# Layer 3 feed-forward: a PSUM pair of its own for the query and key projections, a pinned place for VectorE's rotation, and more, smaller unit parts

## The chip, the cores and the metric

The kernel runs on one core of one Trainium2 chip. The metric is the device time of the whole kernel in microseconds (us); lower is better. The time before is the median of three runs, 2732.9 us, and the three lie between 2726.75 and 2735.28 us. One execution was profiled; it took 2729.0 us, of which 2726.9 us lie between the first and the last instruction (its span).

The engines are named as in the profile: PE is TensorE's matmuls, PEld its weight loads, DVE is VectorE, ACT is ScalarE, POOL is GpSimd, SP is SyncE, which issues DMAs.

## What is computed

The reference is a small network of four layers, each made of a feed-forward block, an attention block and the feed-forward block again. All is float32, with 4 sequences of 512 tokens and 128 features. Only layer 3's feed-forward block is changed. It is itself two transformer layers (`DEPTH = 2`), and it is called twice, before and after layer 3's attention:

```python
def _layer(x, wqkv, qs, ksc, wo, lg, lb, w1, b1, w2, b2):
    h = shift_token(x)                       # upper 64 features come from the token before
    q, k, v = jnp.split(h @ wqkv, 3, axis=-1)    # 8 heads of 64
    q = l2norm(q) * qs; k = l2norm(k) * ksc
    q, k = rotary_xpos(q, k)                 # q * cos * scale + rotate_half(q) * sin * scale
    x = x + local_attention(q, k, v) @ wo    # windows of 64 keys and the 64 before them
    h = shift_token(x)
    h = (h - mean) / sqrt(var + 1e-05) * lg + lb
    a, g = jnp.split(h @ w1 + b1, 2, axis=-1)    # 341 hidden features each
    return x + (a * gelu(g)) @ w2 + b2
```

## The kernel before

`l3_ffn` (lines 1593 to 1901) is one long software pipeline. A **unit** is one of the two transformer layers for one of the four sequences, so a call has 8 units. A **step** is one block of 128 tokens of a unit, so a unit has 4 steps (`TB`) and a call has 32. The loop at lines 1878 to 1886 goes over step numbers n. In each turn it traces six **stages**, each for an older step than the stage before it:

| place | stage | step | what it does |
|---|---|---|---|
| 0 | `project` (1643) | n | PE: q and k into a pair of PSUM banks `p_qk`, v into one bank `pv`. ACT: squares `sq`, copy `v`. DVE: q and k times the cosine table (`t1`, line 1661), two half products with the sine table (`t2`, line 1664), sums of squares `rn` (1666). POOL: inverse root of `rn` (ten small instructions, lines 195 to 205), `t1 + t2` (1668), k times its inverse norm (1669). SP: two DMAs that shift v by half a block (`vb`) |
| 1 | `to_features` (1681) | n - 2 | PE: 8 transposes into a pair `pt_qk`. ACT copies the q half (`qT`), DVE the k half (`kT`, 1693) |
| 2 | `exponentials` (1722) | n - 4 | ACT: 8 exponentials over `s`. DVE: reciprocal `sm`. POOL: `s` times `sm` (1731) |
| 3 | `weights` (1698) | n - 3 | PE: scores into a pair `ps3`. DVE: mask (`s`, 1714), row maximum `nm` (1716) and its scaling (1719) |
| 4 | `turn_weights` (1733) | n - 5 | PE: 8 transposes into a pair `pt3`. ACT copies them (`PT`) |
| 5 | `with_values` (1742) | n - 6 | PE: weights times values into one bank `po3`. DVE copies it (`oT`, 1757) |

The rest of a unit, from the output projection to the second linear layer, is cut into **parts** that are hung between the stages of later steps. `parts` (lines 1867 to 1871) gives for each the step, counted from the unit's first, and the place ahead of which it is traced. `attended`: output projection `pz`, added to `yT` by DVE (1773), then `shift`, which is one copy on ACT and one on DVE into `h2`. `mean`: product `pm`, subtraction on DVE (1782), square on ACT. `variance`: product `pvar`, copy `rs` on DVE (1793), then an inverse root of ten instructions on POOL. `spread`: `rs` into a diagonal matrix `dg` on DVE (1801). `normed`: product `pb` of `dg`, then `h2` scaled on DVE (1811). `hidden` 0, 1 and 2: each two products into a pair `pag`, a GELU on ACT and a product `hh` on DVE (1824). `close_unit`: product `pz2`, added to `yT` on DVE (1836). `leave`: back to token order.

Three things set the order of the work:

- **Pins.** Every PE and ACT instruction of this block goes through `tc.keep_in_program_order`, which places it behind the instruction traced last on the same engine. So PE and ACT run in the order of the code. DVE and POOL instructions of this block are not pinned: a scheduler lays them out when the kernel is compiled, the earliest traced first among those that it takes to be ready. On the chip every engine then works through its own list in order, and an instruction that waits holds up what stands behind it.
- **PSUM rings.** PSUM has 8 banks. `banks(tag + "ps", d=3, m=2)` makes a ring of three pairs for tag `d` (`p_qk`, `pt_qk`, `ps3`, `pt3`, `pag`, in the order of the code) and a ring of two single banks for tag `m` (`pv3`, `pz`, `pm`, `pvar`, `pb3`, `po3` and so on). A product into a ring of three waits until the pair used three before it has been read.
- **Ticks.** Work that other blocks left over is run a piece at a time by `tick()` once after each stage.

Steps 10 to 13 of a call carry the parts of unit 0, steps 14 to 17 those of unit 1, and so on; steps 0 to 9 carry none, and after step 31 only the later stages go on. The last unit's parts follow the loop (`rest`, line 1888), in the second call in two halves.

Of the kernel before, what the change touches and what calls it, by code (L numbers as in the profile page):

```python
# [23 lines left out]
F32, I32 = mybir.dt.float32, mybir.dt.int32  # L24
AF = mybir.ActivationFunctionType
ALU = mybir.AluOpType
AX = mybir.AxisListType

P = 128
# [74 lines left out]
def tile_macaron(ctx, tc, x_in, const_in, vec_in, w0_in, ws_in, ws3_in, w2f_in, w3_in, out):  # L104
    nc = tc.nc
    pool = lambda name, **kw: tc.tile_pool(name=name, bufs=1, **kw)
# [9 lines left out]
    @contextmanager  # L116
    def banks(name, **bufs):
        with pool(name, space=bass.MemoryType.PSUM) as p:
            psum["pool"], psum["bufs"] = p, bufs or {"s": 4, "t": 2, "m": 2}
            yield  # L120

    def bank(tag, name):
        n = 2 if tag == "d" else 1
        return psum["pool"].tile([P, n * 512], F32, tag=tag, name=name, bufs=psum["bufs"][tag])

    def two_banks(name):
# [8 lines left out]
    for b in range(B):  # L135
        nc.sync.dma_start(x[:, ts(b, TB), :], x_in[:, ts(b, TB), :])
        if b == 0:
            a, z = W0.at["ip"]
# [22 lines left out]
    yT = keep.tile([P, B, S], F32, name="yT")  # L161
# [18 lines left out]
    def bcast(ap, n):  # L180

        return ap[:, :, None].to_broadcast([ap.shape[0], ap.shape[1], n])
# [1408 lines left out]


    def l3_ffn(w3, tag, first, rb):
        with pool(tag) as sb, banks(tag + "ps", d=3, m=2):
            units = [(l, b) for l in range(2) for b in range(B)]
            n_steps = TB * len(units)
            u_state = {}
# [5 lines left out]
            def tmp(name):  # L1603
                return rb.tile([P, S], F32, tag="tmp", name=name, bufs=4)
# [3 lines left out]

            def act_copy(dst, src):
                tc.keep_in_program_order(nc.scalar.copy(dst, src))  # L1610

            def pair(name):
                return bank("d", name)
# [5 lines left out]
            def shift(dst, src, at=slice(0, S), u=1):  # L1619

                act_copy(dst[0:64, at], src[0:64, at])
                a = max(at.start, 1)
                if at.start == 0:
                    light(u).memset(dst[64:128, 0:1], 0.0)
                nc.vector.tensor_copy(dst[64:128, a : at.stop], src[64:128, a - 1 : at.stop - 1])
# [17 lines left out]
            def project(step):  # L1643
                u, t = step // TB, step % TB
                l, b = units[u]
                h = u_state[u]["hT"][:, ts(t, P)]
                p = pair("p_qk")
                mm_in_order(p[:, 0:512], h, W(l, "wq"))
                mm_in_order(p[:, 512:1024], h, W(l, "wk"))
                pv = bank("m", "pv3")  # L1650
                mm_in_order(pv, h, W(l, "wv"))

                sq = sb.tile([P, 16, 64], F32, tag="sq", name="sq")
                act(sq.rearrange("p h d -> p (h d)"), p, AF.Square)
                tab = W(l, "tab").rearrange("p (t f i d) -> p t f i d", t=TB, f=2, i=2)[:, t]
                t1 = sb.tile([P, 16, 64], F32, tag="t1", name="t1", bufs=3)
                t2 = sb.tile([P, 16, 64], F32, tag="t2", name="t2")
                by_head = lambda v: v.rearrange("p (i h) d -> p i h d", i=2)
                over = lambda v: v[:, :, None, :].to_broadcast([P, 2, 8, v.shape[2]])
                p3 = p.rearrange("p (h d) -> p h d", d=64)  # L1660
                nc.vector.tensor_mul(by_head(t1), by_head(p3), over(tab[:, 0]))  # L1661
                for half in range(2):
                    a, z = ts(half, 32), ts(1 - half, 32)
                    nc.vector.tensor_mul(by_head(t2[:, :, a]), by_head(p3[:, :, z]), over(tab[:, 1, :, a]))  # L1664
                rn = sb.tile([P, 16], F32, tag="rn", name="rn", bufs=6)
                nc.vector.tensor_reduce(rn, sq, AX.X, ALU.add)
                inverse_root(sb, rn, rn, "ir16", ALU.max, 1e-24, nc.gpsimd)
                nc.gpsimd.tensor_add(t1, t1, t2)  # L1668
                nc.gpsimd.tensor_mul(t1[:, 8:16, :], t1[:, 8:16, :], bcast(rn[:, 8:16], 64))
                v = sb.tile([P, S], F32, tag="v", name="v", bufs=7)  # L1670
                act_copy(v, pv)

                vb = sb.tile([P, S], F32, tag="vb", name="vb", bufs=7)
                nc.sync.dma_start(vb[64:128], v[0:64])
                if t:
                    nc.sync.dma_start(vb[0:64], s_state[step - 1]["v"][64:128])
                else:
                    light(u).memset(vb[0:64], 0.0)
                s_state[step] = {"qk": t1, "rn": rn, "v": v, "vb": vb}

            def to_features(step):
                u, t = step // TB, step % TB
                qk = s_state[step].pop("qk")
                pt = pair("pt_qk")
                for i in range(2):
                    for fc in range(4):
                        transpose_in_order(
                            pt[:, ts(4 * i + fc, P)], qk[:, 8 * i + 2 * fc : 8 * i + 2 * fc + 2, :].rearrange("p h d -> p (h d)")
                        )
                qT = sb.tile([P, 4, P], F32, tag="qT", name="qT", bufs=3)  # L1690
                act_copy(qT.rearrange("p c n -> p (c n)"), pt[:, 0:512])
                kT = u_state[u]["kT"]
                nc.vector.tensor_copy(
                    kT[:, :, 64 + t * P : 64 + (t + 1) * P], pt[:, 512:1024].rearrange("p (c n) -> p c n", n=P)
                )
                s_state[step]["qT"] = qT

            def weights(step):
# [64 lines left out]
            def attended(u, at=whole):  # L1763
                l, b = units[u]
                oT = u_state[u]["oT"]
                n = at.stop - at.start
                pz = bank("m", "pz")
                for fc in range(4):
                    mm_in_order(
                        pz[:, :n], W(l, "wo").rearrange("p (c n) -> p c n", n=D)[:, fc, :], oT[:, fc, at], fc == 0, fc == 3  # L1770
                    )
                z = yT[:, b, :]
                nc.vector.tensor_add(z[:, at], pz[:, :n], z[:, at])
                if at.start == 0:
                    u_state[u]["h2"] = rb.tile([P, S], F32, tag="h2", name="h2", bufs=2)
                shift(u_state[u]["h2"], z, at)

            def mean(u, at=whole):
                h2, n = u_state[u]["h2"], at.stop - at.start
                pm = bank("m", "pm")  # L1780
                mm_in_order(pm[:, :n], onesm, h2[:, at])
                nc.vector.tensor_sub(h2[:, at], h2[:, at], pm[:, :n])
                sq = u_state[u]["sq", at.start] = tmp("sq2")
                act(sq[:, :n], h2[:, at], AF.Square)

# [67 lines left out]
            if first:  # L1853
# [11 lines left out]
                            nc.vector.tensor_add(to, to, pn[:n, i + 1 : i + 2])  # L1865

            parts = [
                (attended, 10, 2), (mean, 10, 4), (variance, 11, 0), (spread, 11, 4), (normed, 12, 0),
                (lambda u: hidden(u, 0), 12, 5), (lambda u: hidden(u, 1), 13, 0), (lambda u: hidden(u, 2), 13, 0),
                (close_unit, 13, 4), (lambda u: leave(units[u][1]) if units[u][0] else None, 14, 0),  # L1870
            ]
            later, last = {}, len(units) - 1
            for u in range(len(units)):
# [3 lines left out]
                later.setdefault((u * TB - 1, 0), []).append((open_unit, u))  # L1877
            for n in range(-2, n_steps + 6):
                for place, (part, lag) in enumerate((
                    (project, 0), (to_features, 2), (exponentials, 4), (weights, 3), (turn_weights, 5), (with_values, 6)  # L1880
                )):
                    for f, u in later.pop((n, place), ()):
                        f(u)
                    if 0 <= n - lag < n_steps:
                        part(n - lag)
                    tick()
            assert not later, later
            rest = [attended, mean, variance, spread, normed]
            rest += [lambda u, at, c=c: hidden(u, c, at) for c in range(3)] + [close_unit, lambda u, at: leave(units[u][1], at)]
            if first:  # L1890
                spare = chain(units[last][1])
                for f in rest:
                    spare(1, lambda f=f: f(last, whole), f is not spread)
                    if f is variance:
                        spare(1, lambda: leave(units[last - 1][1]))
            else:
                for f in rest:
                    for at in (slice(0, S // 2), slice(S // 2, S)):
                        f(last, at)
                    if f is attended:  # L1900
                        leave(units[last - 1][1])


# [177 lines left out]
```

## Time and profile before

| what | us |
|---|---|
| median of the runs | 2732.9 (2726.75 to 2735.28) |
| the profiled execution | 2729.0, span 2726.9 |
| stretch of the first call | 1560 to 1947 of the span: 387.0, PE busy 324.26, DVE 300.67, ACT 259.35, POOL 262.99 |
| stretch of the second call | 2305 to 2727: 422.0, PE busy 360.95, DVE 300.95, ACT 267.57, POOL 260.03 |
| all else | 0 to 1560 and 1947 to 2305 |

The granted clock of PE is 0.94 and 0.93 of full speed in these two stretches. The mean durations that matter, from the groups by form between 2320 and 2640 us:

| engine | instruction | ns |
|---|---|---|
| DVE | `t1` 128x1024, line 1661 | 1224 |
| DVE | half of `t2`, 128x512, line 1664, two of them | 681 |
| DVE | `rn` 1666; mask `s` 1714; `nm` 1716 | 1209; 1217; 1209 |
| DVE | `kT` 1693; `oT` 1757; `yT` add 1773; `dg` 1801 | 681; 686; 690; 693 |
| POOL | `t1 + t2` 1668; k times its norm 1669; `s` times `sm` 1731 | 2366; 1062; 1898 |
| ACT | `sq` 128x1024; `v`, `qT`; `PT`; one exponential (8 in a step) | 1025; 580, 587; 993; 482 |

How to read the profile: a row of the timeline has the start in us, the duration, the engine, line and operation, what it writes and reads, and in brackets the idle time of the engine just before it with what ended that. A row of the waits names who waited for whom, then the total in us, how often, and the longest. A row of the windows gives for each engine the busy time and the number of instructions, then the granted PE clock, the share of DMA time and GB/s.

### The profile page before, as it was taken

To read this page: it belongs to the slowest core of one execution; us is meant where nothing else is said; L and a number is where in the kernel's file an instruction comes from. 1 tells how busy PE (TensorE), PEld (TensorE's weight loads), DVE (VectorE), ACT (ScalarE), POOL (GpSimd) and SP (SyncE) were. 2 spreads that over 40 slices of the span, in tenths; PEclk is the share of its full clock that TensorE was granted. 3 is DMA by queue.
4 is the path that set the end of the run, shared out by engine and by line. 5 is a ranking of instruction groups with operands and counts; after the bars stand their busy time and mean duration, and the time that the engine had idled before them with its cause. 6 is when DMAs were issued, how large, how long until landed. Compare 5 with 4: busy or idle time off the path is not lost. (4 is left out here: it accounts for less than half of the span.)

```text
span 2726.9 us, 49905 instructions
## 1 busy us (share of the span) xinstructions
PE 2191.1 (80%) x18572; PEld 1226.1 (45%) x18572; DVE 1808.4 (66%) x5013; ACT 1267.1 (46%) x3067; POOL 905.4 (33%) x1678
## 2 busy tenths in 40 slices
PE   4277539988779999948666868898899999789888
PEld 2145214443334444438456745555433333455555
DVE  4746487777566777563664487777567775877774
ACT  3054314444333544314332356776525554667764
POOL 1012012233122222213321377766300000877761
PEclk8578769998789999868886889999879999899998
DMA  3053010000000000008104611000000000100000
GB/s 143 0 158 93 0 63 1 1 1 1 1 1 1 1 2 5 5 21 300 37 10 160 200 27 24 21 21 20 1 0 1 1 1 7 28 20 21 22 21 12
DMA packets 33930, 99.31 MB, mean 36 GB/s; under 512 B 6200, under 2 KB 12344, under 8 KB 33176
## 3 DMA queue, kind: packets, MB, share of 16 engines
q1 hardware_dynamic: 30760, 88.03, 10.0%
q0 software_dynamic: 2496, 5.12, 0.8%
q8 instruction: 146, 2.39, 0.4%
q10 hardware_dynamic: 432, 2.98, 0.3%
q14 instruction: 96, 0.79, 0.1%
HBM read 66.88 MB, written 14.55 MB: 30 GB/s over the span
## 5 line engine op out<-in xcount | busy, mean ns | idle before, releaser
L832 ACT ACTIVATE PT<-pk_at 128x512 f32<-128x512 f32 (+3 forms) x768 | 335.2, 488 | 405.4 <-PE pq_at L171 259.3
L171 PE MATMUL pk_at<-qx,km 32*128 32x512 f32 (+3 forms) x1536 | 398.8, 554 | 4.6 <-ACT PT L832 2.7
L804 DVE CUSTOM_DVE_ANT_0 s<-pq_at,cst 128x384 f32<-128x384 f32 (+3 forms) x512 | 249.9, 488 | 96.0 <-PE pq_at L171 42.5
L171 PE MATMUL pq_at<-km,qT 32*128 32x128 f32 (+3 forms) x1024 | 274.0, 500 | 16.0 <-DVE nm L804 12.0
L1607 ACT ACTIVATE s<-s,nm,rn 128x128 f32<-128x128 f32 x512 | 245.5, 482 | 0.9 <-DVE nm L1719 0.7
L835 POOL TENSOR_SCALAR_AFFINE_SELECT PT<-PT 128x256 f32<-128x256 f32 x256 | 104.5, 410 | 388.7 <-ACT PT L832 387.7
L171 PEld LDWEIGHTS pk_at<-qx,km 32*128 32x128 f32 x1536 | 146.7, 190 | 153.3 <-issue 92.9
L171 PE MATMUL po_at<-PT,vh 128*32 128x128 f32 (+3 forms) x2432 | 205.6, 394 | 8.5 <-POOL PT L835 8.4
L806 DVE TENSOR_REDUCE nm<-pq_at 128x1 f32<-128x512 f32 x256 | 165.6, 685 | 57.6 <-PE pq_at L171 57.2
L1668 POOL TENSOR_TENSOR t<-t,t 128x1024 f32<-128x1024 f32 x64 | 151.8, 2372 | 123.4 <-DVE t L1664 123.1
L171 PE MATMUL pq_at<-km,t 32*128 32x512 f32 x512 | 175.0, 670 | 1.6 <-DVE nm L806 1.2
L168 PE MATMUL pt_y<-ident,y 128*128 128x128 f32 x224 | 52.3, 362 | 132.2 <-DVE y L225 104.9
L171 PE MATMUL p_qk<-w,hT 128*128 128x512 f32 x256 | 141.9, 682 | 8.8 <-DVE t L1664 6.0
L254 ACT COPY yT<-pt_y 128x512 f32<-128x512 f32 x56 | 32.8, 585 | 239.1 <-PE pt_y L168 238.6
L168 PE MATMUL pt<-ident,s 128*128 128x128 f32 x640 | 93.0, 293 | 62.0 <-POOL s L1731 38.9
L1731 POOL TENSOR_TENSOR s<-s,sm 128x1024 f32<-128x1024 f32 x64 | 121.6, 1901 | 49.1 <-DVE sm L1730 41.0
L171 PEld LDWEIGHTS po_at<-PT,vh 128*32 128x32 f32 x2432 | 53.8, 109 | 173.3 <-issue 119.8
L171 PEld LDWEIGHTS pq_at<-km,qT 32*128 32x128 f32 x1024 | 110.2, 189 | 46.6 <-DVE nm L804 26.8
L1607 ACT ACTIVATE sq<-p_qk 128x1024 f32<-128x1024 f32 x64 | 65.6, 1026 | 118.4 <-PE p_qk L171 65.8
L168 PEld LDWEIGHTS pt<-ident,s 128*128 128x128 f32 x640 | 78.2, 150 | 93.7 <-POOL s L1731 48.1
L1661 DVE TENSOR_TENSOR t<-p_qk,w 128x1024 f32<-128x1024 f32 x64 | 78.2, 1223 | 55.7 <-ACT sq L1607 55.6
L1349 DVE SCALAR_TENSOR_TENSOR hT<-pa,w,sg 128x128 f32<-128x128 f32 x184 | 51.9, 345 | 85.4 <-ACT sg L1348 63.6
(435 smaller groups left out, 5167.6 us busy)
## 6 DMA issues: line engine op xcount, KB each, us to landing
w<-in_w2f_dram SPq DMA_DIRECT2D x46, 836.0 KB, 6.2
vb<-v SPq DMA_DIRECT2D x112, 128.0 KB, 2.2
skew<-qe SPq DMA_DIRECT2D x16, 512.0 KB, 3.0
rel<-skew SPq DMA_DIRECT2D x64, 128.0 KB, 3.5
w<-in_w_dram SPq DMA_DIRECT2D x1, 4147.0 KB, 12.5
w<-in_w_dram SPq DMA_DIRECT2D x1, 3200.0 KB
od<-o SPq DMA_DIRECT2D x46, 64.0 KB, 5.1
yd<-y SPq DMA_DIRECT2D x8, 256.0 KB, 2.3
```

Of the source, the lines that this page charges most:

```text
L168: return nc.tensor.transpose(dst, src, ident[: src.shape[0], : src.shape[0]])
L171: tc.keep_in_program_order(nc.tensor.matmul(dst, lhsT=lhsT, rhs=rhs, start=start, stop=stop))
L254: by_order(nc.scalar.copy(yT[:, b, :], pt))
L804: nc.vector.tensor_tensor_reduce(s[:, :nk], pq[:, :nk], causal[:, S - nk :], 1.0, -BIG, ALU.add, ALU.max, to)
L806: nc.vector.tensor_reduce(to, pq, AX.X, ALU.max)
L832: by_order(nc.scalar.activation(PT[:, i, q0:], pk[:, q0:], AF.Exp, scale=SC8))
L835: nc.gpsimd.affine_select(d, d, pattern=[[0, 2], [1, P]], base=0, channel_multiplier=-1, compare_op=ALU.is_ge, fill=0.0)
L1349: nc.vector.scalar_tensor_tensor(hT[s][:, c, :], pa[:, ts(c, P)], b1[:, c : c + 1], sg, ALU.add, ALU.mult)
L1607: tc.keep_in_program_order(nc.scalar.activation(*args, **kw))
L1661: nc.vector.tensor_mul(by_head(t1), by_head(p3), over(tab[:, 0]))
L1668: nc.gpsimd.tensor_add(t1, t1, t2)
L1731: nc.gpsimd.tensor_mul(s, s, bcast(sm, P))
```

## The change

PSUM's eight banks are dealt out anew: one pair with tag `w` for `p_qk` alone, a ring of two pairs `d` for the other four users, and two single banks as before. The last part of `project`, from the half products `t2` on, becomes a function `rotate` that is run by a stage of its own, `rotated`, for the same step n, at place 2, behind `to_features` and behind any part hung at place 2. `t1`, `kT`, the two `t2` and `rn` are pinned on DVE. In `rotate` the POOL sum `t1 + t2` is traced ahead of the inverse root. There are now seven places, so `tick()` runs seven times in a step. `attended` gives its shift to a part `shifted`, `mean` its square to a part `squared`, and the parts get new places:

```diff
-        n = 2 if tag == "d" else 1
+        n = 2 if tag in "dw" else 1
...
-        with pool(tag) as sb, banks(tag + "ps", d=3, m=2):
+        with pool(tag) as sb, banks(tag + "ps", w=1, d=2, m=2):
...
+            in_order = tc.keep_in_program_order
...
-                p = pair("p_qk")
+                p = bank("w", "p_qk")
...
-                nc.vector.tensor_mul(by_head(t1), by_head(p3), over(tab[:, 0]))
-                for half in range(2):
-                    a, z = ts(half, 32), ts(1 - half, 32)
-                    nc.vector.tensor_mul(by_head(t2[:, :, a]), by_head(p3[:, :, z]), over(tab[:, 1, :, a]))
-                rn = sb.tile([P, 16], F32, tag="rn", name="rn", bufs=6)
-                nc.vector.tensor_reduce(rn, sq, AX.X, ALU.add)
-                inverse_root(sb, rn, rn, "ir16", ALU.max, 1e-24, nc.gpsimd)
-                nc.gpsimd.tensor_add(t1, t1, t2)
-                nc.gpsimd.tensor_mul(t1[:, 8:16, :], t1[:, 8:16, :], bcast(rn[:, 8:16], 64))
                 v = sb.tile([P, S], F32, tag="v", name="v", bufs=7)
                 act_copy(v, pv)
+                in_order(nc.vector.tensor_mul(by_head(t1), by_head(p3), over(tab[:, 0])))
+
+                def rotate():
+                    for half in range(2):
+                        a, z = ts(half, 32), ts(1 - half, 32)
+                        in_order(nc.vector.tensor_mul(by_head(t2[:, :, a]), by_head(p3[:, :, z]), over(tab[:, 1, :, a])))
+                    rn = s_state[step]["rn"] = sb.tile([P, 16], F32, tag="rn", name="rn", bufs=6)
+                    in_order(nc.vector.tensor_reduce(rn, sq, AX.X, ALU.add))
+                    nc.gpsimd.tensor_add(t1, t1, t2)
+                    inverse_root(sb, rn, rn, "ir16", ALU.max, 1e-24, nc.gpsimd)
+                    nc.gpsimd.tensor_mul(t1[:, 8:16, :], t1[:, 8:16, :], bcast(rn[:, 8:16], 64))
...
-                nc.vector.tensor_copy(
+                in_order(nc.vector.tensor_copy(
                     kT[:, :, 64 + t * P : 64 + (t + 1) * P], pt[:, 512:1024].rearrange("p (c n) -> p c n", n=P)
-                )
+                ))
...
                 nc.vector.tensor_add(z[:, at], pz[:, :n], z[:, at])
+
+            def shifted(u, at=whole):
                 if at.start == 0:
                     u_state[u]["h2"] = rb.tile([P, S], F32, tag="h2", name="h2", bufs=2)
-                shift(u_state[u]["h2"], z, at)
+                shift(u_state[u]["h2"], yT[:, units[u][1], :], at)
...
                 nc.vector.tensor_sub(h2[:, at], h2[:, at], pm[:, :n])
+
+            def squared(u, at=whole):
+                h2, n = u_state[u]["h2"], at.stop - at.start
                 sq = u_state[u]["sq", at.start] = tmp("sq2")
                 act(sq[:, :n], h2[:, at], AF.Square)
...
-                (attended, 10, 2), (mean, 10, 4), (variance, 11, 0), (spread, 11, 4), (normed, 12, 0),
-                (lambda u: hidden(u, 0), 12, 5), (lambda u: hidden(u, 1), 13, 0), (lambda u: hidden(u, 2), 13, 0),
-                (close_unit, 13, 4), (lambda u: leave(units[u][1]) if units[u][0] else None, 14, 0),
+                (attended, 10, 2), (shifted, 10, 4), (mean, 11, 2), (squared, 11, 4), (variance, 11, 6), (spread, 12, 2),
+                (normed, 12, 4), (lambda u: hidden(u, 0), 12, 6), (lambda u: hidden(u, 1), 13, 0),
+                (lambda u: hidden(u, 2), 13, 1), (close_unit, 13, 5), (lambda u: leave(units[u][1]) if units[u][0] else None, 14, 0),
...
-                    (project, 0), (to_features, 2), (exponentials, 4), (weights, 3), (turn_weights, 5), (with_values, 6)
+                    (project, 0), (to_features, 2), (rotated, 0), (exponentials, 4), (weights, 3), (turn_weights, 5), (with_values, 6)
...
-            rest = [attended, mean, variance, spread, normed]
+            def both(f, g):
+                return lambda u, at: (f(u, at), g(u, at))
+
+            rest = [both(attended, shifted), both(mean, squared), variance, spread, normed]
```

The places in the new list count with `rotated` in it: 0 `project`, 1 `to_features`, 2 `rotated`, 3 `exponentials`, 4 `weights`, 5 `turn_weights`, 6 `with_values`.

More of the change, by code (lines that the diff above doesn't have):

```diff
@@ L1678, in project, with rotated @@
                     light(u).memset(vb[0:64], 0.0)
-                s_state[step] = {"qk": t1, "rn": rn, "v": v, "vb": vb}
+                s_state[step] = {"qk": t1, "v": v, "vb": vb, "rotate": rotate}
+            def rotated(step):
+                s_state[step].pop("rotate")()
             def to_features(step):
@@ L1899, in l3_ffn @@
                         f(last, at)
-                    if f is attended:
+                    if f is rest[0]:
                         leave(units[last - 1][1])
```

## Prediction

> **What bounds the kernel now.** The change touches only the two calls of `l3_ffn`, so I read those stretches, first by windows, then by PE's waits, then the timelines of the engines that PE waits for. In the windows, after the slice's length, come busy time and count of PE, PEld, DVE, ACT and POOL, then PE's granted clock:
>
> ```profile
> 2448.00:2453.00 5.00, 4.97 (x14) 2.67 (x15) 0.57 (x2) 2.10 (x3) 3.73 (x11) 0.66 0.09 19
> 2453.30:2500.20 46.90, 43.38 (x385) 25.78 (x384) 35.85 (x52) 33.94 (x90) 32.94 (x67) 0.97 0.09 21
> 2500.20:2546.90 46.70, 43.40 (x410) 26.47 (x412) 35.65 (x52) 34.72 (x91) 33.01 (x67) 1.00 0.09 21
> ```
>
> The last two rows are one unit (four steps) each, from a `dg` step to the next. PE is busy 43.4 of 46.8 us: PE bounds a unit, and at most 3.4 us of idle time plus a slow-clock stretch can be won. The first row lies just behind such idle time: the clock falls to 0.66 over 5 us, which loses 5 x 0.34 = 1.7 us. Without that, PE's own work is 43.4 - 1.7 = 41.7 us, and 40.8 if I add up its groups at their shortest (p_qk 1.75, pv 0.86, pt_qk 0.9, ps 1.04, pt 0.97, po 1.08, four times = 26.4; pz 3.53, pm 0.9, pvar 0.92, pb 0.96, pag 3 x 1.76, pz2 2.7 = 14.3). PE's waits between 2320 and 2640:
>
> ```profile
> PE pt L168 <- POOL s L1731: 11.7, 7, 4.5
> PE pt L168 <- DVE t L1664: 9.4, 8, 2.6
> PE pvar L171 <- ACT sq L1607: 7.3, 6, 1.3
> PE p_qk L171 <- DVE t L1664: 3.5, 2, 2.5
> PE pag L171 <- DVE kT L1693: 2.3, 5, 0.6
> ```
>
> The second, fourth and fifth rows are the ring of three: `pt3` takes the pair of this step's `p_qk` and waits for its last rotation, `pag` takes that of `pt_qk` and waits for `kT`. The first row is data from POOL. Now the layer norm's chain, on DVE and then on POOL:
>
> ```profile
> 2496.05 0.16 DVE L1793 COPY rs<-pvar 128x4 f32<-128x4 f32 x1 [1.39 <-PE pvar L171]
> 2499.54 0.69 DVE L1801 SCALAR_TENSOR_TENSOR dg<-ident,rs 128x512 f32<-128x512 f32 x1 [3.33 <-POOL rs L205]
> 2500.15 1.22 DVE L1661 TENSOR_TENSOR t<-p_qk,w 128x1024 f32<-128x1024 f32 x1
> ```
>
> ```profile
> 2487.72 2.37 POOL L1668 TENSOR_TENSOR t<-t,t 128x1024 f32<-128x1024 f32 x1 [0.91 <-DVE t L1664]
> 2490.17 0.30 POOL L195 TENSOR_SCALAR ir<-rn 128x16 f32<-128x16 f32 x1
> ...
> 2493.23 1.04 POOL L1669 TENSOR_TENSOR t<-t,rn 128x512 f32<-128x512 f32 x1
> ...
> 2494.75 1.90 POOL L1731 TENSOR_TENSOR s<-s,sm 128x1024 f32<-128x1024 f32 x1
> 2496.74 0.23 POOL L195 TENSOR_SCALAR ir<-rs 128x4 f32<-128x4 f32 x1
> ...
> 2499.31 0.20 POOL L205 TENSOR_TENSOR rs<-ir 128x4 f32<-128x4 f32 x1
> ...
> 2502.71 2.37 POOL L1668 TENSOR_TENSOR t<-t,t 128x1024 f32<-128x1024 f32 x1 [2.43 <-DVE t L1664]
> ```
>
> A step's block on POOL is sum 2.37, root 3.06 (2490.17 to 2493.23), product 1.1, `s` times `sm` 1.95: 8.5 us in a row. The layer norm's root (2496.74 to 2499.51, 2.8 us) now falls into POOL's only long pause, ahead of the next sum, because `variance` is traced ahead of a step's `project`.
>
> **The ring.** In steps without `pag` the new rings ask for less: `pt3` waits for `pt_qk`'s readers in place of `p_qk`'s; `ps3` and `pt_qk` wait for what they waited for; `p_qk` waits for its own rotation of the step before. This takes away up to 9.4 + 3.5 + 2.3 = 15.2 us in this window of about seven units. With `pag` it asks for more: `pag` 0 waits for `ps3` (mask `s`), `pag` 1 for `pt3`, `pag` 2 for `pag` 0, the next `ps3` for `pag` 2.
>
> **DVE's order.** Now t1, t2, t2, rn, kT. Then t1, kT, any part at place 2, t2, t2, rn. kT comes 2.5 us sooner, the rotation 0.6 later. But a pin sets t2 behind the DVE instruction traced last. In steps 10, 11 and 12 of a unit that is the `yT` add, the mean's subtraction and `dg`. Behind the waiting one stand t2, rn and the mask; POOL's whole block waits for t2. Tracing the sum ahead of the root costs nothing: the rows show it running first already. Moving `v`'s copy costs nothing on ACT (its order stays sq, v); the two `vb` DMAs on SP's queue land in 2.2 us and are needed six steps, some 70 us, later; without that cover they would cost those 2.2 us. The seventh tick only moves leftover work by part of a step, in each call's first ten steps: -2 to +2 us, I take 0.
>
> **A unit walked through**, zero at step 10's `p_qk`, with the durations above; ACT's sq starts 0.2 us behind `p_qk` and takes 1.02.
>
> Step 10: PE p_qk to 1.75, pv 2.6, pt_qk 3.5, pz 7.05, ps 8.1, pt 9.05, po 10.1. DVE: t1 3.0 to 4.2, kT 4.8, then idle until pz is done; `yT` add 7.25 to 7.9, t2 9.15 (5.4 in the old order), rn 10.3, copy of `h2` 0.45, mask, nm, small ones, oT, copy of `hT`: 14.4. POOL: block from 9.3 to 17.85.
>
> Step 11: PE p_qk 11.85, pv 12.7, pt_qk 13.65, pm 13.9 (oT frees its bank) to 14.8, ps 15.85, pt waits for `s` times `sm` until 17.9, to 18.9, pvar 19.8, po 20.9. ACT's square of `h2` stands behind qT and eight exponentials (18.3 to 18.9): it just fits. DVE: t1 14.4 to 15.6, kT 16.2, subtraction 16.85, t2 18.1. POOL: sum 20.6, root 23.7, product 24.8, `s` times `sm` 26.7. `rs` is ready at 21.6, behind all of these: root 26.7 to 29.5.
>
> Step 12: PE p_qk 22.65, pv 23.5, pt_qk 24.45, then pb waits for `dg` (29.5 to 30.2): **5.8 us idle**. pb 31.2, ps 32.2, pt 33.2. DVE: t2 31.4, rn 32.5, `h2` 33.2, mask 34.4; so `pag` 0 waits 1.2 for its pair, to 36.2, po 37.3.
>
> Step 13: `pag` 1 39.05, p_qk 40.8, pv 41.65, `pag` 2 43.4, pt_qk 44.3; GELU and `hh` 2 free the pair of ps at 45.1 (0.8 wait), 46.15, pz2 48.85, pt 49.8, po 50.9.
>
> So a unit takes 40.8 + 0.25 + 2.05 + 5.8 + 1.2 + 0.8 = 50.9 us. The rotation's late end also nears step 11's `p_qk`, which needs the pair back: 9.15 against 10.1, so its cover is 0.95 us; past that it adds one for one.
>
> **PE's clock**, where rule and row differ. The Trainium skill, page "TensorE: Matmul & The Clock Gate", section "Why this matters for your kernels", says that matmul bursts keep the full clock if no idle gap exceeds about 3 us. By it the old gap of 1.27 us ahead of pvar costs only itself, and the new one of 5.8 us starts a half-clock stretch that is new. By the row at 2448 the small gap (with 0.4 us just before) brought a slow stretch already, so the old unit pays 1.7 us too and the new one swaps it. By the row I add 1.7 for the stretch behind pb, less what hides under the 1.2 us that `pag` 0 waits, and something for the 2.05 us gap: 1.0. By the rule alone it would be 1.7 - 1.2 = 0.5. Bounds: 0 (all under waits) to 2.5 (two stretches, half hidden). I take 1.0: 51.9 us a unit.
>
> **The unknown: where POOL's list puts the layer norm's root.** No row shows it behind a full block. Traced last, it should be last. But a memset on POOL, traced later than a root, once ran inside it (2507.74), so the list can slip it in. Best: mixed into step 11's root, ahead of product and `s`: 3.0 us sooner, a unit of 47.9 to 48.3. Worst: last, with 2.5 us of clock, 53.4. I take last, since all else of the block is ready sooner and traced sooner.
>
> **Sum.** 51.9 - 46.8 = +5.1 us a unit. Six units in each call (steps 12, 16 to 32) get the wait, five of them whole and the sixth about half: 11 in all, +56 us. Steps 0 to 9: waits for t2's pair go (2.5 us once a call at most), but POOL's 8.5 us block already sets those steps of about 8.3 us: -1 each. The tail: old waits for `s` times `sm` (up to 3.3 us) pass into the wait for pb: -3 to +3, I take 0. +54 on the profiled execution's 2729.0 gives 2783; on the median 2732.9, which lies 3.9 above it, 2787.
>
> **Rivals.** (1) The root slips in: 48.3 - 46.8 = 1.5 x 11 = +17, 2750. For it: the memset. Against: the root's own next step is traced sooner. 18%. (2) Faster: the parts' inputs come in time, and the ring's gain is kept. It decides at `dg` done by 24.45 in the walk, so `rs` must find POOL free at 21. Then a unit is PE's 41.7 plus one wait of 0.8 for POOL's `s`: -4.3 x 11 = -47, 2686. For it: PE's and ACT's order leaves 4.6 us of work between pvar and pb for a chain of 0.2 + 2.8 + 0.7 and hand-offs. Against: POOL is busy 33 of 46.8 us, and its block starts late in just these steps. 13%. (3) No net change: POOL free at `rs`, but the other waits (0.25, 2.05, 0.6 at pb, 1.2, 0.8) and half a slow stretch stay: 46.5 + 0.5 = 47.0, 2735. 11%. Root last: 55%; worse than my walk (both slow stretches, a late pair in step 11): 3%. DVE as bound: 35.8 us of work plus 2.45 idle behind pz is under every unit above.
>
> What a measurement tells from no change is 0.3%, 8 us. Faster 0.13; same 0.11; slower 0.55 + 0.18 + 0.03 = 0.76. The range runs from just under no change to the walk's worst, 6.6 x 11 = +73 with +9 for tails, 2815.
>
> **What would show it.** The profile after should have PE pb waiting on DVE `dg` about 5 us, twelve times; DVE `yT` add waiting on pz about 2.4 us; POOL's `ir<-rs` behind `s<-s,sm` and next to no pause ahead of it; no wait of pt on t2; some on `hh` at ps. Wrong, if `ir<-rs` stands ahead of the step's block, or if units are shorter than 46.8 us.

## The result, and the profile after

The changed kernel takes 2804.6 us (median of four runs, 2802.88 to 2805.91), against 2731.92 for the kernel before beside it on the same chip (2726.75 to 2735.28): a ratio of 1.0258, 95% interval 1.0237 to 1.028. The predicted 2787 was 18 us low, inside the range. The profiled execution has a span of 2803.8 us, 76.9 more than before. Measured from the start of one `p_qk` to that of another, those 76.9 us lie as follows, rounded: eight whole units (steps 12 to 28 of both calls) +51.4, the rest of the calls behind step 28 (about three units more, with what follows the first call) +19.4, all that lies ahead of step 12 +6.0.

The windows of the changed kernel, two units of the second call in one row each, the busy columns as before:

```profile
2448.30:2501.90 53.60, 44.97 (x385) 26.66 (x384) 37.00 (x52) 33.83 (x88) 32.87 (x66) 0.95 0.08 18
2501.90:2555.50 53.60, 45.06 (x366) 27.39 (x366) 36.92 (x52) 33.84 (x88) 32.85 (x66) 0.91 0.08 18
```

A unit has grown from 46.8 to 53.6 us with the same work in it: DVE, ACT and POOL are as busy as before within 1.5 us, and PE's busy time has grown only by slow clock (means over four units: busy time less what the slow clock takes is 41.6 us before and 41.5 after). PE's waits in 320 us of the second call, 2360 to 2680 (the rows of before were from a window of the same length, as far behind the start of the call):

```profile
PE pb L171 <- DVE dg L1813: 17.8, 5, 4.2
...
PE pvar L171 <- ACT sq L1607: 8.3, 5, 1.7
```

The first row is new: `pb` waits for `dg`. The other, `pvar`'s wait for its square, has grown by 1 us, from 1.3 to 1.7 at its longest. Over the whole run `pb` waits 49.6 us for `dg` in 14 waits (longest 6.5), against 1.1 us in 2 before. The old wait of `pt` for the rotation's `t2` has shrunk to 1.6 us here (9.4 before). How the new one comes about is read from DVE, then from POOL, of the same unit:

```profile
2501.60 0.15 DVE L1805 COPY rs<-pvar 128x4 f32<-128x4 f32 x1
...
2501.84 0.68 DVE L1764 COPY oT<-po 128x512 f32<-128x512 f32 x1
2509.99 0.69 DVE L1813 SCALAR_TENSOR_TENSOR dg<-ident,rs 128x512 f32<-128x512 f32 x1 [7.47 <-POOL rs L205]
2510.60 1.22 DVE L1665 TENSOR_TENSOR t<-p_qk,w 128x1024 f32<-128x1024 f32 x1
```

```profile
2498.32 2.37 POOL L1673 TENSOR_TENSOR t<-t,t 128x1024 f32<-128x1024 f32 x1 [0.93 <-DVE t L1670]
...
2503.76 1.04 POOL L1675 TENSOR_TENSOR t<-t,rn 128x512 f32<-128x512 f32 x1
2504.76 1.90 POOL L1738 TENSOR_TENSOR s<-s,sm 128x1024 f32<-128x1024 f32 x1
2506.59 0.52 POOL L1682 MEMSET vb<- 64x512 f32 x1
2507.20 0.23 POOL L195 TENSOR_SCALAR ir<-rs 128x4 f32<-128x4 f32 x1
...
2513.69 2.36 POOL L1673 TENSOR_TENSOR t<-t,t 128x1024 f32<-128x1024 f32 x1 [3.73 <-DVE t L1670]
```

`rs` is copied at 2501.60, but POOL is in the middle of step 11's block: root, product, `s` times `sm` and a memset. The layer norm's root starts at 2507.20, 5.5 us late. Meanwhile DVE stands at `dg` for 7.47 us with `t1` of the next step behind it, and POOL in its turn then lacks that step's rotation for 3.73 us.

### The profile page after: what moved, and what is told of

It is laid out like the page before. It is cut to its first block, busy times and chain, and to the rows that moved or that the text cites. A ratio compares the mean times of both kernels' runs of the same rounds, so it can differ in the third digit from the quotient of the medians.

```text
span 2803.8 us, 49961 instructions
## 1 busy us (share of the span) xinstructions
PE 2219.4 (79%) x18572; PEld 1243.0 (44%) x18572; DVE 1825.5 (65%) x5013; ACT 1270.3 (45%) x3067; POOL 905.0 (32%) x1678
## 4 chain that ended last, share of the span: by engine, by line
PE 54%; DVE 27%; POOL 9%; ACT 4%; issue 4%; DMA 1%; another core or an unknown queue 0%; DVEq 0%; POOLq 0%; ACTq 0%; SPq 0%
PE pk_at L171 10%; PE po_at L171 5%; PE pa L171 4%; PE pag L171 3%; PE pq_at L171 3%; PE pz L171 3%; PE po L171 3%; PE p_qk L171 2%; PE pe L171 2%; DVE t L1670 2%; PE pv L171 2%; PE pg L171 2%; POOL t L1673 2%; DVE y L1053 1%; DVE t L1665 1%
## 5 line engine op out<-in xcount | busy, mean ns | idle before, releaser
L171 PE MATMUL po_at<-PT,vh 128*32 128x128 f32 (+3 forms) x2432 | 206.5, 395 | 7.0 <-POOL PT L835 6.8
L171 PE MATMUL p_qk<-w,hT 128*128 128x512 f32 x256 | 152.6, 726 | 28.5 <-DVE t L1670 22.0
L168 PE MATMUL pt_y<-ident,y 128*128 128x128 f32 x224 | 52.7, 365 | 127.7 <-DVE y L225 98.7
L1738 POOL TENSOR_TENSOR s<-s,sm 128x1024 f32<-128x1024 f32 x64 | 121.4, 1897 | 56.5 <-DVE sm L1737 50.7
L171 PE MATMUL pag<-h,w 128*128 128x512 f32 (+3 forms) x204 | 96.8, 605 | 13.2 <-DVE h L1823 6.6
```

Source lines behind the costliest of these rows:

```text
L168: return nc.tensor.transpose(dst, src, ident[: src.shape[0], : src.shape[0]])
L171: tc.keep_in_program_order(nc.tensor.matmul(dst, lhsT=lhsT, rhs=rhs, start=start, stop=stop))
L1738: nc.gpsimd.tensor_mul(s, s, bcast(sm, P))
```

## The experiments

My theory: the parts now put the layer norm's root behind a full POOL block, and that wait, with the slow clock around it, makes most of the loss. First rival: the ring of two costs the time, since its pairs are given back late. Second rival: the clock costs it, and waits matter only through the clock. Third: the pins on DVE.

The kernel before ran beside each group of kernels on the same chip. Its medians are 2722.25 us (beside ring_only to root_dve), 2720.37 (rotation_only to warm_pb), 2720.39 (after_ring3 and the two shift kernels) and 2732.35 (ring3_dve), and a ratio is taken within its group. The unit, PE's idle time in it and what the clock takes (the sum of time by one less the granted clock) are means over four units of the second call in the profiled execution:

| kernel | ratio to before, 95% interval | unit | PE idle | clock |
|---|---|---|---|---|
| before | 1 | 46.9 | 4.0 | 1.3 |
| the change | 1.0258 [1.0237, 1.028] | 53.6 | 8.3 | 3.8 |
| ring_only | 1.0213 [1.0194, 1.0231] | 51.6 | 8.1 | 2.2 |
| places_only | 1.0101 [1.0084, 1.0118] | 49.1 | 5.6 | 2.0 |
| old_places | 1.018 [1.0161, 1.0198] | 51.2 | 6.5 | 3.4 |
| root_dve | 1.0166 [1.0145, 1.0186] | 50.7 | 5.7 | 3.6 |
| rotation_only | 1.0025 [1.001, 1.004] | 46.7 | 4.3 | 0.9 |
| places_dve | 1.003 [1.0018, 1.0042] | 47.9 | 4.5 | 1.9 |
| unpinned | 1.0197 [1.0172, 1.0222] | 52.5 | 7.5 | 3.6 |
| warm_pb | 1.0327 [1.0296, 1.0357] | 54.9 | 6.1 | 4.0 |
| after_ring3 | 1.0205 [1.0182, 1.0228] | 52.7 | 7.2 | 4.1 |
| shift_later | 1.0052 [1.0035, 1.0069] | 48.7 | 5.3 | 2.1 |
| shift_pb_later | 1.02 [1.0177, 1.0224] | 52.7 | 7.5 | 4.2 |
| ring3_dve | 1.0093 [1.0076, 1.011] | 49.5 | 5.4 | 2.6 |

**ring_only: the kernel before with the new rings alone.**

```diff
-        with pool(tag) as sb, banks(tag + "ps", d=3, m=2):
+        with pool(tag) as sb, banks(tag + "ps", w=1, d=2, m=2):
-                p = pair("p_qk")
+                p = bank("w", "p_qk")
```

> The kernel before with the PSUM rings alone changed (p_qk in a pair of its own, a ring of two for the rest); DVE's order and the parts' places as before. Theory A, that the loss is the layer norm's root behind POOL's block: 2720 to 2735, since waits of pt, p_qk and pag on the old ring (15 us in seven units) go and waits on the new one come; PE's pb shows no wait on dg. Theory B, that the loss is the smaller ring and the lone pair: 2755 or more, with most of the 12 us by which the first call's first twelve steps became longer.

Measured: 2782.51 us, a unit of 51.6. PE's waits in its four units (206.5 us) begin with this row:

```profile
PE pt L168 <- DVE kT L1693: 25.8, 8, 3.8
```

`pt3` takes the pair of `pt_qk`, so it waits for `kT`, and in the old order of DVE `kT` stands behind `t1`, both `t2` and `rn`: 6.46 us a unit, more than all waits on `t2` and POOL before. Without `kT` put forward, the ring of two is a loss by itself. My "asks for less" was wrong for the ring alone, and the time is in the range of theory B. It does not show that the change loses its time in the same way: there the same wait is 1.04 us a unit.

**places_only: the kernel before with the parts split and at their new places, and an empty place where `rotated` would be.**

```diff
-                (attended, 10, 2), (mean, 10, 4), (variance, 11, 0), (spread, 11, 4), (normed, 12, 0),
+                (attended, 10, 2), (shifted, 10, 4), (mean, 11, 2), (squared, 11, 4), (variance, 11, 6), (spread, 12, 2),
...
-                    (project, 0), (to_features, 2), (exponentials, 4),
+                    (project, 0), (to_features, 2), (None, 0), (exponentials, 4),
```

> The kernel before with the new parts at their new places (an empty seventh place stands where the rotation's stage would be); ring of three, DVE's rotation unpinned and ahead of kT. Theory A: the places alone bring the wait, pb waits on dg 3 us or more in each unit, and the time is 2770 to 2800. Theory B: 2745 or less. Theory C, that DVE's pins are needed for the loss: 2735 to 2760, with pb waiting under 2 us.

Measured: 2751.77 us, a unit of 49.1. The wait of `pb` appears with no ring and no pin changed:

```profile
PE pb L171 <- DVE dg L1806: 8.4, 4, 3.7
```

But it is 2.1 us a unit, and in the change 3.8. Theory A had expected 3 us or more, and 2770 us at least. The places alone make a unit longer by 2.2 us, the whole change by 6.6.

**old_places: the changed kernel with its split parts back in the old order.** Only the list of places is edited.

```diff
-                (attended, 10, 2), (shifted, 10, 4), (mean, 11, 2), (squared, 11, 4), (variance, 11, 6), (spread, 12, 2),
-                (normed, 12, 4), (lambda u: hidden(u, 0), 12, 6), (lambda u: hidden(u, 1), 13, 0),
-                (lambda u: hidden(u, 2), 13, 1), (close_unit, 13, 5),
+                (attended, 10, 3), (shifted, 10, 3), (mean, 10, 5), (squared, 10, 5), (variance, 11, 0), (spread, 11, 5),
+                (normed, 12, 0), (lambda u: hidden(u, 0), 12, 6), (lambda u: hidden(u, 1), 13, 0),
+                (lambda u: hidden(u, 2), 13, 0), (close_unit, 13, 5),
```

> The changed kernel with the parts put back to the order they had before (shift and square right behind their inputs, variance ahead of a step's project, spread a place ahead of with_values' neighbour, normed ahead of project); new ring and pinned rotation kept. Theory A: the root runs in POOL's pause again, pb does not wait on dg, units of 46 to 47.5 us, 2735 to 2750 with the first call's ramp still 12 us long. Theory B or C: 2780 or more.

Measured: 2770.97 us, between the two ranges, and a unit of 51.2, so the new places cost 2.4 us a unit here. No wait on `dg` is left, but others stand where it was:

```profile
PE pt L168 <- DVE kT L1700: 9.7, 8, 2.0
PE pag L171 <- DVE s L1721: 9.2, 4, 2.3
```

The second row is the ring's price in the steps with `pag`: `pag` 0 needs the pair of `ps3`, and so the mask.

**root_dve: the changed kernel with every layer norm's root on DVE.**

```diff
-                eng = nc.vector if u == len(units) - 1 else nc.gpsimd
+                eng = nc.vector
```

> The changed kernel with the layer norm's inverse root on DVE for every unit in place of POOL (eight instructions on DVE in place of ten on POOL); all else as in the changed kernel. Theory A: dg no longer waits for POOL's queue, the wait of pb on dg falls from 3.6 us to under 1 us, DVE's own wait of 6 to 7.5 us ahead of dg falls to under 2 us, units fall from 53.2 to 48 to 49.5 us, 2755 to 2770. Theory B: 2800, as DVE only gets more work. Theory C, DVE's list as such: 2785 to 2800.

Measured: 2769.66 us, a unit of 50.7. In its four units this row is left:

```profile
PE pb L171 <- DVE dg L1813: 1.8, 3, 0.9
```

The wait of `pb` for `dg` falls from 3.78 to 0.45 us a unit, the unit by 2.9 of the 6.6, and the loss of the whole run from 2.6% to 1.7%. So POOL's queue is shown to carry more than a third of the loss, but not most of it, as my theory had it. `pag`'s waits rise from 1.2 to 1.9 us, and the clock takes nearly as much as in the change (3.6 against 3.8). The unit is still 3.8 us longer than before: by the table 1.7 of that is idle time and 2.3 slow clock.

**rotation_only: the pinned stage alone, with a ring of three and the old places.**

```diff
-        with pool(tag) as sb, banks(tag + "ps", w=1, d=2, m=2):
+        with pool(tag) as sb, banks(tag + "ps", d=3, m=2):
```

(in old_places, with `p_qk` again from `pair`.)

> The kernel before with the rotation's own stage and DVE's pins alone: ring of three pairs, parts at the places they had. Theory A, in its second form (units lose about 2.5 us by the root behind POOL's block, and about 3.9 by ring and rotation together): with kT ahead of t2, pt3 still takes p_qk's pair and waits for a t2 that is 0.6 us later, so units of 47 to 48.5 us and 8 to 18 us over before. Theory B, the ring of two is the cost and the rotation order is a gain: at or under before. Theory C, the pins are the cost: 25 us or more over before.

Measured: 2726.81 us, 0.25% above before, a unit of 46.7. The stage and its pins, with the old ring and places, cost and gain next to nothing. Against old_places only the rings differ: 46.7 against 51.2 us; `pag`'s wait for the mask adds 2.3 and the clock 2.6, and small waits fall.

**places_dve: places_only with the root on DVE**, the same edit as in root_dve.

> The kernel before with the new parts at their new places, and the layer norm's inverse root on DVE in place of POOL. The places alone cost 29.5 us, with pb waiting 2.3 us on dg in each unit. Theory A: that wait and its slow clock go, the step of the three matmul parts falls from 16.5 to 13 us or less, the kernel is 0 to 15 us under before. Theory B (the places cost by themselves, as pvar waits 2 us for the square): 15 us or more over before.

Measured: 2727.18 us, a unit of 47.9. The places' loss falls from 1.0% to 0.3%, and the wait for `dg` from 2.1 to 0.8 us a unit: what the places cost in the old order was mostly the root behind POOL's block.

**unpinned: the changed kernel with no pins on DVE.**

```diff
-            in_order = tc.keep_in_program_order
+            in_order = lambda i: i
```

> The changed kernel with the pins on DVE taken off (t1, kT, t2, t2 and rn traced in the same order and the same stage); rings and places kept. Theory C: t2 no longer stands behind the yT add and dg, POOL's block starts 2 to 3 us sooner, units fall from 53.2 to under 50.5 us, 30 us or more under the changed kernel. Theory A and B: within 12 us of the changed kernel, gained mostly in the first call's first twelve steps, where t1 is pinned behind layer norms of other sequences.

Measured: 2773.96 us, a unit of 52.5, still with 3.4 us of wait for `dg`. The pins cost 1.1 us of the 6.6, less than the 3 us that theory C had expected.

**warm_pb: the changed kernel with PE kept busy while `pb` waits.** Four more products, which nobody reads, stand ahead of `pb`.

```diff
+                if at is whole:
+                    idle = bank("m", "idle")
+                    for _ in range(4):
+                        mm_in_order(idle, onesm, cst[:, :S])
                 pb = bank("m", "pb3")
```

> The changed kernel with four products that nobody reads ahead of each whole unit's pb, eight matmul instructions of 0.43 us, about 3.5 us of PE work where PE waits 3.6 us for dg. If the slow clock behind that wait costs nothing, the time is that of the changed kernel to 5 us; if it costs the 1.7 us a unit that I left out of the walk for the most part, units fall by 1 to 2 us and the kernel by 10 to 25 us, with less slow clock behind pb.

Measured: 2809.81 us, a unit of 54.9. The first row of PE's waits in four units:

```profile
PE pag L171 <- DVE s L1721: 9.1, 4, 2.4
```

The wait of `pb` fell from 3.78 to 0.4 us a unit, but `pag` now waits 2.29 for the mask, and the clock takes 4.0 in place of 3.8. Work in the gap did not bring the clock back, and the kernel fits neither of the two expectations. It speaks against the second rival in its simple form (the wait of `pb` slows the clock); it doesn't settle what does.

**after_ring3: the changed kernel with a ring of three**, `p_qk` in it, by the edit of rotation_only.

> The changed kernel with the ring of three pairs put back (p_qk in it again); pinned rotation and new places kept. If ring and places add up as the runs so far say (ring of two 3.9 to 4.6 us a unit, places 2.2), units fall from 53.6 to 49 to 50 us, pb still waits 2 to 4 us on dg, and the kernel is 35 to 50 us under the changed one, 25 to 40 over before. If the ring's loss only hides behind the wait for dg (theory A as I predicted it), units stay above 52 us and less than 20 us are won.

Measured: 2778.76 us, a unit of 52.7: 0.9 less. From that and root_dve I formed a reading of two limits, each hiding the other, and tested it last.

**shift_later and shift_pb_later: the kernel before with one piece of the change.** The first traces the shift as a part of its own behind the exponentials, and the second also moves `normed` from (12, 0) to (12, 4).

```diff
-                (attended, 10, 2), (mean, 10, 4),
+                (attended, 10, 2), (shifted, 10, 3), (mean, 10, 4),
```

> The kernel before with one edit: the shift into h2 is a part of its own, traced behind the exponentials of the same step and ahead of weights. ACT then does not wait 3.6 us for the yT add ahead of eight exponentials. If that wait is what makes PE wait 1.27 us ahead of pvar and then run slow, pvar's wait goes, units fall from 46.9 to 44.5 to 46 us, 15 to 30 us under before; pm may wait 0.3 us longer for h2. If PE's other waits take its place: within 8 us of before.

> As the one with the later shift, and normed moved from ahead of project to between the scores and the transposes of the same step, so that pb's 0.96 us of PE work lies where PE waits 0.9 us for the weights from POOL. If it fills that wait: a further 0.5 to 1 us a unit, 5 to 10 us. If h2 then comes too late for the first hidden product: no gain over the later shift, or up to 10 us slower, with pag waiting on h2.

Measured: 2737.06 us and 2777.98 us, units of 48.7 and 52.7. PE's largest waits in four units of each:

```profile
PE pt L168 <- DVE t L1664: 17.0, 8, 3.3
```

```profile
PE pag L171 <- DVE nm L1719: 14.8, 4, 3.7
PE pt L168 <- DVE t L1664: 13.2, 4, 3.3
```

In the first the wait of `pvar` for its square (1.27 us a unit) is gone, and the ring's wait of `pt` for `t2` has grown from 1.23 to 4.24. In the second PE's `pag` stands behind a mask and maximum that come later. Moving a piece passes the wait on. Both kernels are slower than either of their expectations had it. None of the kernels is faster than the one before; rotation_only and places_dve come within 0.3%.

**ring3_dve: both limits taken away**, the edits of after_ring3 and root_dve together.

> The changed kernel with both suspected limits taken away at once: the ring of three back, and the layer norm's root on VectorE. Alone, the ring of three brought the unit from 53.6 to 52.7 us and the root on VectorE brought it to 50.7. Theory of two limits, each of which hides the other (the wait of pb for dg, and behind it the ring's waits at pt and pag): with both gone the unit falls to 47.5 to 48.5 us, near the 47.9 of the new places with the root on VectorE in the old rotation order, and the ratio to before is 1.003 to 1.009. Rival, the rotation pinned behind the parts costs time of its own at these places, whatever ring and root: the unit stays between 49.5 and 51, no wait on dg over 0.5 us a unit, but waits of pt or pag for the late rotation or mask, ratio 1.010 to 1.017. Second rival, the two gains simply add to each other: 53.6 - 0.9 - 2.9 = 49.8, ratio 1.011.

Measured: 2755.57 us, a unit of 49.5. The reading of two limits fell: the unit misses its 47.5 to 48.5, and the sum of the two single gains (49.8) fits. The first rival, a cost of the rotation itself, had a range that begins at 49.5, so it is not ruled out, but its signs are not there: `pb` still waits 0.65 us a unit for `dg`, and `pag` waits for the scaled `h2` (1.46) and not for the mask. The timelines of PE and of DVE in step 11 show why giving back the ring gave so little:

```profile
2516.03 1.06 PE L168 MATMUL pt<-ident,s 128*128 128x128 f32 x8 [0.99 <-DVE kT L1700]
```

```profile
2515.20 0.68 DVE L1700 COPY kT<-pt_qk 128x512 f32<-128x512 f32 x1
2515.80 0.68 DVE L1791 TENSOR_TENSOR h<-h,pm 128x512 f32<-128x512 f32 x1
2516.40 1.28 DVE L1670 TENSOR_TENSOR t<-p_qk,w 128x512 f32<-128x512 f32 x2
```

`pt` starts as `kT` ends, with `t2` still to come. So it has not taken the pair of `p_qk`, as a ring of three in the order of use would give it. This is no single case. In steps 6 to 31 of the two calls `pt` starts before the last `t2` of the same turn has ended in 33 of 52 turns of after_ring3, and in none of the kernel before; in after_ring3 it never starts before `kT` has ended, and in the kernel before it does, by up to 1.6 us.

So "the pair used three before", as I described the ring, does not hold once the rotation's readers are traced behind `kT`: `pt` then follows `pt_qk`, as in the change. That `p_qk` gets its own pair back, so that a ring of three deals itself out as one pair for `p_qk` and two for the rest, fits the traces (in after_ring3 it never starts until 1.0 us after its last `t2`), but they do not prove it, and the rule by which the pairs are dealt out was not tested. On this reading the ring of after_ring3, rotation_only and ring3_dve differs from the change's only in the steps with `pag`. The exchange is worth 0.9 us a unit at the new places and 4.5 at the old.

## Why the prediction was right, and where its sizes were off

**The late root: right, place and time.** The prediction had the root last in POOL's block, `dg` ready 9.3 us behind step 12's `p_qk` (30.2 less 20.9). In the unit shown it is 9.4 (2510.68 less 2501.30). `yT`'s add waits 2.13 us for `pz` (2.4 was named). The closeness of 9.4 to 9.3 is in part luck: counted from step 11's `p_qk`, `dg` is ready at 20.8 us and not at 20.1, and step 11 itself is longer by as much. root_dve shows the price by taking it away: 2.9 us a unit. Reading POOL's own order of work, and not its share of the span, found this. Step by step, the walk gave 10.1 and 11.85 us for steps 10 and 13; measured are 10.2 and 11.8 in four units of the second call. Steps 11 and 12 together were 28.95 us plus 1.0 for the clock; measured are 30.4 to 31.6.

**The gap at `pb`: 5.8 us in the walk, 3.78 measured, and the clock is the other side of it.** The time at which `dg` is ready was right, and what PE does until then was not. These are PE's rows, with step 11's `p_qk` first and step 12's last:

```profile
2489.87 1.98 PE L171 MATMUL p_qk<-w,hT 128*128 128x512 f32 x4
...
2496.52 1.07 PE L168 MATMUL pt<-ident,s 128*128 128x128 f32 x8 [0.99 <-DVE kT L1700]
...
2501.30 3.59 PE L171 MATMUL p_qk<-w,hT 128*128 128x512 f32 x4
```

Step 12's `p_qk` runs at half clock and takes 3.59 us in place of 1.98, so PE comes to `pb` later and waits less. The windows of the same unit, cut at the changes of the clock:

```profile
2501.30:2504.70 3.40, 3.40 (x9) 1.34 (x6) 1.21 (x4) 0.00 (x0) 2.67 (x9) 0.53 0.00 0
2504.70:2511.80 7.10, 2.99 (x13) 1.54 (x11) 1.81 (x3) 5.91 (x19) 4.42 (x13) 0.98 0.08 18
2511.80:2515.20 3.40, 3.40 (x40) 3.00 (x40) 3.40 (x6) 0.00 (x0) 1.51 (x1) 0.50 0.00 0
```

One slow stretch lies ahead of the wait and is partly hidden by it, the second lies behind it and costs. Not every unit has this form: in the next one a single slow stretch of 6.8 us begins at 2552.73, `pb` then waits only 2.67 us, no slow stretch follows the wait, and the unit (50.8 us) is shorter than its neighbours (55.2). I had counted one stretch, half hidden, with 2.5 us as the bound; the clock takes 3.75 us a unit. Waits and clock together are 12.1 us against 11.1 in the walk (10.1 + 1.0), so two wrong sizes nearly cancel.

**The baseline of the difference: wrong.** The walk took PE's own work as 40.8 us, from the shortest groups, and set the sum against a measured unit. By the same reckoning (busy time less what the clock takes) PE's work is 41.6 us before and 41.5 after. So the walk came out 0.7 us a unit too short: waits and clock make 1.0 and this base 0.7, and the unit is 53.6 instead of 51.9.

**The count of units: right.** All that lies behind step 12 of both calls, 51.4 + 19.4 = 70.8 us, is 6.4 us for each of eleven; I had 5.1 by 11 = 56.

**DVE's order in step 12, and `pag`'s wait: size right, cause wrong.** The walk had `t1` and `kT` of step 12 done ahead of `dg`, `h2` scaled 3.0 us behind it and the mask 4.2, and `pag` 0 waiting 1.2 us for the mask. But `dg` is not pinned, and DVE's list puts it first. So `t1` and `kT` stand behind it too, and `h2` and the mask end 4.7 and 5.85 us after it. And `pag` 0 does not wait for the mask, as these rows of the next unit show:

```profile
2568.23 0.74 DVE L1823 SCALAR_TENSOR_TENSOR h<-h,w,pb 128x512 f32<-128x512 f32 x1
2568.89 1.22 DVE L1721 TENSOR_TENSOR s<-ps,cst 128x1024 f32<-128x1024 f32 x1
2569.11 1.96 PE L171 MATMUL pag<-h,w 128*128 128x512 f32 x4 [1.31 <-DVE h L1823]
```

`pag` starts as `h2` is done, and the mask ends only at 2570.11. It is so in five of ten units of the two calls. In the other five `pag` starts 0.05 us after ACT's copy `PT` has ended, so it has the pair of `pt3`. The mean wait is 1.15 us, and that 1.2 was named is luck. In old_places and warm_pb the mask is what ends last.

**Other small waits: mixed.** `ps` on `hh` 0.68 (0.8 named) is right. `pt`'s wait of 2.05 us for POOL's `s` is not there: the list let `s` of step 10 into a root (at 2491.53, behind that root's first instruction), and `pt` waits 0.99 us for `kT`. Slipping in, my first rival's mechanism, did occur, but for `s` and not for the layer norm's root. And `pvar` waits 1.65 us for ACT's square, where the walk said that it just fits.

**The ring: wrong.** A gain of up to 15.2 us in the window was named. ring_only shows a loss without `kT` put forward, and rotation_only shows that with `kT` put forward nothing is left for the pair of its own to add: `pt` no longer waits for `t2` there. What remained of the change's ring was its price at `pag` (0.9 us a unit against after_ring3), and one more at a place where I had seen a gain: `p_qk`'s waits for its own `t2` did not go but grew from 6.0 us in 3 waits to 22.0 in 9 over the whole run, all of the 9 in steps 1 to 5 of a call. With the ring of three in after_ring3 they are 1.6.

**The ramp: open.** I took -1 us a call ahead of step 12. The first call gave +9.0 (-2.8 on the way to its first `p_qk`, +11.8 from there on), the second -3.0, in spite of `p_qk`'s waits in both. The 9.0 can't be put down to the change. root_dve and warm_pb have the same order of work as the changed kernel on PE, DVE, ACT and POOL up to step 11 of that call, by the names in the trace, and yet they reach step 12 at 1672.3 and 1665.2 us, where the changed kernel comes at 1681.7 and the one before at 1672.7. What drives them apart I don't know. It is a reason to compare units here, and not whole runs alone.

**The rivals tested.** Taken one at a time from the kernel before, the losses add up to the whole (places +2.2, rings +4.7, stage -0.3, against +6.6 together), but not because they are the same losses: ring_only's 4.7 is a wait of `pt` for `kT` of 6.46 us, and the change has 1.04 of it. In another order the shares are others: the rings 4.5 at the old places and 0.9 at the new, the places 2.2, 2.4 or 6.0. So the 6.6 us can't be dealt out among the three. Why the places cost +2.2 in the old order and +6.0 with the pinned stage (rotation_only to after_ring3) is read from the rows above: DVE stands at `dg`, and the rotation and POOL's next sum stand behind it. The pins are 1.1 us in the change itself; the rest is argued, with no kernel that separates it. The slow clock, 2.5 us a unit more than before in the change, is measured, but no kernel here takes it away while it leaves the waits.

## What to carry to other kernels

Before a step of a pipeline is moved, follow its input through the queue of the engine that will work on it: ten small instructions of 2.8 us, placed behind an 8.5 us block, cost 2.9 us of a unit here, as root_dve shows. A ring of buffers has to be read together with the order in which its readers are traced, and both together decide who waits. Parts of a loss that add up are not thereby its parts: look whether each wait is still there in the whole. A difference must have the same base on both sides: model both units, or measure both.

## What the runs showed of the hardware

- **Slow clock after short gaps.** Two gaps of 0.99 and 1.65 us within 4 us (`pt` and `pvar` above) were followed, 2 us on, by a stretch at 0.53 of the clock. The Trainium skill's figure in "TensorE: Matmul & The Clock Gate", section "Why this matters for your kernels", of gaps over about 3 us, doesn't cover this; the row decides. The slow stretches here are 3.4 or 6.8 us long. What sets them off, the sum of idle time or its place, was not settled: the two gaps come in every unit, but in the next one the stretch begins at 2552.73, as the second gap ends.
- **DVE beside POOL.** With the root on DVE the ten instructions become eight, of 0.15 to 0.18 us where POOL is at small ones. Where they meet POOL's large products they last longer, in these traces until the product is done: in ring3_dve the last step of the root took 1.00 us and ended at 2524.32, beside a product from 2523.26 to 2524.30. `dg`, 0.69 us elsewhere, took 2.35 from 2524.36 on and ended 0.55 us behind POOL's `s` times `sm`, which ran from 2524.26 to 2526.16. So moving a root to the other engine did not free it from POOL's block altogether.
